# One decoder layer: the seven late shared experts in a chain, their sums beside them, and one routed tile moved to the last list

## The chip, the cores and the metric

The kernel runs on one core of a Trainium2 chip. The metric is device time in microseconds (us) from start to end of one execution. TensorE (PE in the profile) multiplies matrices. VectorE (DVE), ScalarE (ACT) and GpSimd (POOL) do elementwise work. SyncE (SP) starts most of the transfers. Each engine works through its own list of instructions in order and waits on semaphores for the others.

## The reference, cut to what matters

64 sequences of 128 positions with 256 features go through one layer. A state-space mixer and a retention-style cross-attention come first, each followed by a residual sum and a layernorm. A mixture of experts is last:

```python
shared = down(silu(x @ shared_gate) * (x @ shared_up))      # for every token
probs = sigmoid(x @ router + bias); the two best of 8 experts per token, weights scaled to sum 1
combined = sum over those two of weight * down_e(silu(x @ gate_e) * (x @ up_e))
out = layernorm(x + shared + combined)
```

Every expert has an inner width of 512. All data are float32.

## The kernel before, in words

The work is cut into 16 **groups** of four sequences (512 tokens). A group's features lie with the tokens on the partitions (`x2`, 128 x 4 x 256) and turned (`x2T`, features on the partitions).

**Routing.** `route` (L910) computes the router for a group, ranks the experts and writes each token's row twice into `xs`, a buffer in device memory with a section for each of the 8 experts. That is done with eight indirect transfers from GpSimd's queue (L992). From the counts so far `tile_list` (L1039) makes a list of **tiles**: 256 (or in the last batch 128) rows of one expert. There are 78 tiles in five batches, `BATCHES`: 9, 16 and 16 tiles are listed after groups 4, 8 and 12; 16 full tiles and 21 half tiles after the last group.

**One routed tile** (`one_tile`, L1215): `fetch` (L1134) copies the tile's list entry on GpSimd, loads its rows from `xs` and, if the expert is another one than the buffer holds, its 1.5 MB of weights, both through SyncE's queue. There are three weight buffers (`NW`). `rows_turned` (L1156) transposes the rows on TensorE, `hidden` (L1172) makes the gate and up products, and `down` (L1198) the down products. The down of tile i stands behind the hidden of tile i+1 (`waiting`), and its rows leave for `ys` by an indirect transfer from GpSimd (L1208). After the tile, `room[0] = i + NW` (L1226) lets the next tile be fetched.

**The shared expert** of a group (`shared`, L1003): four chunks of 128 inner features. Each chunk has a gate product and an up product in a PSUM bank of the pool `gu` (three banks), SiLU on ScalarE (L1015) and a multiplication on VectorE (L1016), which gives `hc`. Then come two down products, each over two sequences, also in `gu`, and an add on VectorE for each (L1024). Float32 products are two TensorE passes, so a chunk is 8 instructions in the profile, and a group is 32 (128x512) for gate and up and 32 (128x256) for down. Groups 7 to 13 (`LATE`) do it at the end (`late_shared`, L1454). The others do it earlier, and put x plus the shared part in `x2_rows`.

**The sum** (`combine`, L1230): one 1 MB load of the two routed rows of each token (`picked`, three buffers), two adds of 128x1024 on VectorE (L1239), and `layernorm` (L551): statistics on VectorE for each sequence (L557, L558), variance plus epsilon (L560), a power of -1/2 on GpSimd (L562), shift (L564), four scalings on ScalarE (L567), and a store of 512 KB (L1242).

**The order of the work** is written out by a small planner inside the kernel. `abreast` (L1247) takes several generators. Each says, at each step, where it stands (a position) and how long it should rest. The one with the lowest position that is not resting goes next. The clock, `work[0]`, counts TensorE's time by the kernel's own rates. `placed` (L1265) turns the work done and the rests into a position. There are three such runs, one after the other:

1. L1448: attention of all groups, routing, early shared experts and 41 routed tiles. `per_tick` (L1407) says how many tiles stand beside each group: four beside each of the ticks 13 to 16.
2. L1470: the other 37 tiles, padding rows for `xs` (`fill_behind`, L1100: eight indirect transfers from GpSimd, then seven from SyncE), and the shared expert of group 15.
3. L1487: the seven late shared experts (`all_shared`) beside the 16 sums (`all_sums`, L1476). The nine early groups are summed first, the seven late ones after them, in the order in which their shared parts are made. A late sum uses a tile `x2s_late` for the group.

The order of instructions on an engine is not wholly that of the code: a ready instruction can be brought forward. In the trace two products of group 7's shared expert lie in the middle of the last routed tile's down (1856.48 us).

Of the kernel before, what the change touches and what calls it, by code (L numbers as in the profile page):

```python
# [26 lines left out]
CF = FF // P  # L27
NE = 8
NF = NE + 1
GB = 4  # L30
T = GB * L
# [13 lines left out]
LATE = range(7, 14)  # L45
# [464 lines left out]
def _shared_decay(ctx, K):  # L510
    tc, nc = K.tc, K.tc.nc
    NG = K.x.shape[0] // GB
    x, ctxT, ffn, out = K.x, K.ctxT, K.ffn, K.out
    ident, mhalf, gam, bet, w_in_s, cw, cb, w_x_s = (
        K.ident, K.mhalf, K.gam, K.bet, K.w_in_s, K.cw, K.cb, K.w_x_s
    )
# [7 lines left out]
    ring = ctx.enter_context(tc.tile_pool(name="ring", bufs=3))  # L524
    tiles = ctx.enter_context(tc.tile_pool(name="tiles", bufs=2))
    small = ctx.enter_context(tc.tile_pool(name="small", bufs=4))
    dram = ctx.enter_context(tc.tile_pool(name="dram", bufs=2, space=bass.MemoryType.DRAM))
    pm = ctx.enter_context(tc.tile_pool(name="pm", bufs=5, space=bass.MemoryType.PSUM))
    gu = ctx.enter_context(tc.tile_pool(name="gu", bufs=3, space=bass.MemoryType.PSUM))
# [21 lines left out]

    def layernorm(dst, src):

        mv = small.tile([P, GB, 2], F32, name="mv")
        for b in range(GB):
            st = small.tile([P, nc.vector.BN_STATS_DIM], F32, name="st")
            nc.vector.bn_stats(st, src[:, b, :])  # L557
            nc.vector.bn_aggr(mv[:, b, :], st)  # L558
        var = small.tile([P, GB], F32, name="var")
        nc.vector.tensor_scalar(var, mv[:, :, 1], EPS, None, ALU.add)  # L560
        rstd = small.tile([P, GB], F32, name="rstd")
        nc.gpsimd.tensor_tensor(rstd, var, mhalf, ALU.pow)  # L562
        shift = small.tile([P, GB], F32, name="shift")
        nc.vector.scalar_tensor_tensor(shift, mv[:, :, 0], -1.0, rstd, ALU.mult, ALU.mult)  # L564
        yield 4.2
        for b in range(GB):
            nc.scalar.activation(  # L567
                dst[:, b, :], src[:, b, :], AF.Identity, bias=shift[:, b : b + 1], scale=rstd[:, b : b + 1]
            )
# [430 lines left out]
            nc.sync.dma_start(out=x2T_rows[g], in_=x2T.rearrange("p k t -> p (k t)"))  # L1000
        st["x2T"] = x2T

    def shared(x2, x2T, x2s):  # L1003

        wg = shared_w[:, 0:SZ].rearrange("p (k i) -> p k i", k=KD)
        wu = shared_w[:, SZ : 2 * SZ].rearrange("p (k i) -> p k i", k=KD)
        wd = shared_w[:, 2 * SZ :].rearrange("p (c h) -> p c h", c=CF)
        hid = []
        for c in range(CF):
            psg = gu.tile([P, T], F32, name="gu")  # L1010
            project(psg, wg, c * P, x2T)
            psu = gu.tile([P, T], F32, name="gu")
            project(psu, wu, c * P, x2T)
            hc = ring.tile([P, T], F32, name="hc", bufs=4)
            nc.scalar.activation(hc, psg, AF.Silu)  # L1015
            nc.vector.tensor_tensor(hc, hc, psu, ALU.mult)  # L1016
            hid.append(hc)
            yield 0.3 if c < CF - 1 else 2.0
        for j in range(GB // 2):
            ps = gu.tile([P, 2, D], F32, name="gu")  # L1020
            for i in range(2):
                b = 2 * j + i
                project_rows(ps[:, i, :], [h[:, b * L : (b + 1) * L] for h in hid], wd, slice(0, D))
            nc.vector.tensor_tensor(  # L1024
                x2s[:, 2 * j : 2 * j + 2, :], x2[:, 2 * j : 2 * j + 2, :], ps, ALU.add
            )
            yield

    def early_shared(g, st):
        yield from shared(st["x2"], st["x2T"], st["x2"])  # L1030
        nc.sync.dma_start(out=x2_rows[g].rearrange("p (b d) -> p b d", d=D), in_=st["x2"])

    def load_rows(g):
        xts.append(xts.pop(0))
        t = xts[-1]
        nc.sync.dma_start(out=t.rearrange("p b d -> p (b d)"), in_=x2_rows[g])
        return t

    def tile_list(k):  # L1039

# [188 lines left out]

    def combine(g, x2s):  # L1230

        y = late.tile([P, GB, 2, D], F32, name="picked", bufs=3)
        nc.sync.dma_start(
            out=y, in_=ys[g * GB * 2 * L : (g + 1) * GB * 2 * L, :].rearrange(
                "(b p k) d -> p b k d", p=P, k=2)
        )
        yield 1.0
        for k in range(2):
            nc.vector.tensor_tensor(x2s, x2s, y[:, :, k, :], ALU.add)  # L1239
        yield 3.0  # L1240
        yield from layernorm(x2s, x2s)
        nc.sync.dma_start(out=out[g * GB : (g + 1) * GB].rearrange("b l d -> l b d"), in_=x2s)  # L1242
        yield 3.0


# [90 lines left out]
    for side in range(2):  # L1336
# [3 lines left out]
        b0, half = 0, L // 2  # L1340
        while half >= Q:
# [4 lines left out]
            b0, half = 2 * nb, half // 2  # L1346
        ps = pm.tile([KB, P], F32, name="pm")
# [6 lines left out]
    SZ = KD * FF  # L1354
    shared_w = const.tile([P, 3 * SZ], F32, name="shared_w")
# [51 lines left out]
    per_tick = {}  # L1407
    for k, (groups, first, n, _) in enumerate(BATCHES[:-2]):
        ticks = range(groups + 1, BATCHES[k + 1][0] + 1)
        for j, t in enumerate(ticks):  # L1410
            per_tick[t] = n * (j + 1) // len(ticks) - n * j // len(ticks)
    def until(ready, at):
        while not ready():
            yield at, 0.5
# [36 lines left out]

    late = ctx.enter_context(tc.tile_pool(name="late", bufs=1))

    def late_shared(g):  # L1454
        x2 = load_rows(g)
        x2T = two.tile([P, KD, T], F32, name="x2T")
        nc.sync.dma_start(out=x2T.rearrange("p k t -> p (k t)"), in_=x2T_rows[g])
        yield 4.0
        x2s = late.tile([P, GB, D], F32, name="x2s_late", bufs=len(LATE))
        yield from shared(x2, x2T, x2s)  # L1460
        sums.append((g, x2s))

    sums = []
    def other_tiles():
        begin = listed[0]
        for i in range(begin, NT):
# [4 lines left out]
        (other_tiles(), True), (placed(fill_behind(), 0.0, 23.0, 0.25), True),  # L1471
        (placed(early_shared(NG - 1, states[NG - 1]), 0.0, 23.0, 0.15), True),
    )
    sums += [(g, None) for g in range(NG) if g not in LATE]

    def all_sums():  # L1476
        for i in range(NG):
            while not sums:
                yield i / NG, 1.0
            g, x2s = sums.pop(0)  # L1480
            yield from placed(combine(g, load_rows(g) if x2s is None else x2s), i / NG, 12.0, 1 / NG)

    def all_shared():
        for i, g in enumerate(LATE):
            yield from placed(late_shared(g), i / len(LATE), 27.0, 1 / len(LATE))

    abreast((all_shared(), True), (all_sums(), True))  # L1487

# [184 lines left out]
```

## Time and profile before

| what | value |
|---|---|
| three runs | 2025.27, 2032.85, 2033.28 us; median 2032.85 |
| the profiled execution | 2031.02 us |
| its span, first to last instruction | 2029.2 us |
| mean granted TensorE clock | 0.979 |
| TensorE busy, whole span | 1887.0 us (93%) |
| VectorE busy, whole span | 990.6 us (49%) |
| run 2 (tiles of the last list) | about 1512 to 1858 us |
| run 3 (late shared experts, sums) | about 1858 us to the end |

A view "by stretches" gives for each stretch of the span the busy time of each engine, the granted clock, the busy share of the transfer engines and their rate. A "group" is all instructions of one line, engine and operation on the same tiles, with the number of them, the time of one, and what ended the idle time before them. A "timeline" lists instructions in order of time. Its columns are start, duration, engine, line, operation, output and input, count, and in brackets the idle time before the first of them with what ended it. The "chain" is followed back from the last instruction.

### The profile page before, as it was taken

The page shows a single profiled execution, that of the slowest core. Times are in us where ns is not written, and L with a number is a line of the kernel's source. Part 1 is how long each engine was busy: PE and PEld are TensorE (multiplying, and loading weights), DVE is VectorE, ACT ScalarE, POOL GpSimd, SP SyncE. Part 2 cuts the span into 40 slices and gives each one's busy share as a digit, 9 for nine tenths or more (in the row PEclk, how much of TensorE's full clock was granted, in tenths as well). Part 3 has the DMA queues.
Part 4 walks back from the last instruction along what each step waited for, and adds up shares of the span by engine and source line. Part 5 has one row for each costly group of instructions (what it writes and reads, how often), then busy time and mean ns, then how long its engine had stood idle before and what let it go on. Part 6 is the DMA issues. An engine that isn't in the chain of part 4 may idle for free. (4 is left out here: it accounts for less than half of the span.)

```text
span 2029.2 us, 26056 instructions
## 1 busy us (share of the span) xinstructions
PE 1887.0 (93%) x9252; PEld 1402.0 (69%) x9252; DVE 990.6 (49%) x2400; ACT 757.6 (37%) x1248; POOL 466.7 (23%) x699
## 2 busy tenths in 40 slices
PE   4889998999999979999999899999997999899996
PEld 2655666686868657767777677777775888787553
DVE  3666676655555564555555555554440111012574
ACT  4355344343334434444535353525221222222332
POOL 3021221230303121313131222222223222222110
PEclk9899999999999989999999999999998999999999
DMA  4111121420404142512331342322114332443772
GB/s 145 28 55 44 45 73 34 159 72 23 135 26 133 54 146 75 177 54 83 92 100 54 125 136 95 96 94 75 53 52 164 127 120 71 167 159 124 252 269 79
DMA packets 96308, 206.40 MB, mean 102 GB/s; under 512 B 22344, under 2 KB 59848, under 8 KB 91048
## 3 DMA queue, kind: packets, MB, share of 16 engines
q1 hardware_dynamic: 73048, 149.37, 22.8%
q0 software_dynamic: 17616, 52.46, 7.6%
q10 hardware_dynamic: 5504, 2.81, 0.5%
q8 instruction: 75, 1.23, 0.3%
q14 instruction: 65, 0.53, 0.1%
HBM read 207.33 MB, written 58.60 MB: 131 GB/s over the span
## 5 line engine op out<-in xcount | busy, mean ns | idle before, releaser
L543 PE MATMUL gu<-rows_T,routed_w 128*128 128x256 f32 (+1 forms) x2496 | 504.4, 355 | 15.6 <-DMA routed_w<-in_ffn_dram 15.5
L543 PEld LDWEIGHTS gu<-rows_T,routed_w 128*128 128x128 f32 x2496 | 421.1, 193 | 79.7 <-issue 30.3
L1192 DVE TENSOR_TENSOR hid<-hid,gu 128x512 f32<-128x512 f32 x135 | 92.5, 685 | 395.9 <-PE gu L543 327.6
L543 PE MATMUL pm<-routed_w,hid 128*128 128x256 f32 x1080 | 259.2, 386 | 0.3 <-issue 0.2
L543 PE MATMUL pm<-xnT,w_in_s 128*128 128x512 f32 x512 | 242.8, 599 | 5.2 <-ACT xnT L580 2.6
L543 PE MATMUL gu<-x2T,shared_w 128*128 128x512 f32 x512 | 229.9, 595 | 1.2 <-DVE hc L1016 1.2
L1208 POOL DMA_INDIRECT ys<-rows_out,to x135 | 138.2, 1024 | 380.7 <-ACT rows_out L1207 327.4
L543 PEld LDWEIGHTS pm<-routed_w,hid 128*128 128x128 f32 x1080 | 200.7, 193 | 27.7 <-issue 3.3
L628 DVE SCALAR_TENSOR_TENSOR xc<-pm,cw,xc 128x508 f32<-128x508 f32 (+2 forms) x192 | 141.0, 740 | 68.4 <-ACT xc L623 65.4
L543 PEld LDWEIGHTS gu<-x2T,shared_w 128*128 128x128 f32 x512 | 94.8, 190 | 108.9 <-issue 101.7
L543 PEld LDWEIGHTS pm<-xnT,w_in_s 128*128 128x128 f32 x512 | 96.0, 193 | 91.2 <-issue 76.4
L567 ACT ACTIVATE x<-x,shift,rstd 128x256 f32<-128x256 f32 x132 | 70.7, 591 | 202.3 <-DVE shift L564 202.3
L562 POOL TENSOR_TENSOR rstd<-var,mhalf 128x4 f32<-128x4 f32 x64 | 68.3, 1068 | 330.1 <-DVE var L560 166.5
L1191 ACT ACTIVATE hid<-gu 128x512 f32<-128x512 f32 x135 | 80.4, 596 | 152.1 <-PE gu L543 135.7
L1207 ACT ACTIVATE rows_out<-pm,wt 128x256 f32<-128x256 f32 x135 | 58.0, 472 | 189.6 <-PE pm L543 168.8
L543 PE MATMUL gu<-shared_w,hc 128*128 128x256 f32 x512 | 117.0, 382 | 7.4 <-DVE hc L1016 7.3
L543 PE MATMUL pm<-w_out_s,sz 128*128 128x256 f32 x512 | 117.0, 382 | 4.3 <-DVE sz L784 3.8
L543 PEld LDWEIGHTS gu<-shared_w,hc 128*128 128x128 f32 x512 | 95.7, 190 | 28.6 <-DVE hc L1016 11.8
L543 PEld LDWEIGHTS pm<-w_out_s,sz 128*128 128x128 f32 x512 | 95.8, 190 | 25.9 <-DVE sz L784 7.6
L992 POOL DMA_INDIRECT xs<-x,index x64 | 66.7, 1042 | 174.0 <-issue 78.8
L623 ACT ACTIVATE xc<-pm,cb,cw 128x512 f32<-128x512 f32 x64 | 49.7, 777 | 117.9 <-PE pm L543 117.9
L640 ACT ACTIVATE sz<-pm 128x512 f32<-128x512 f32 x64 | 37.9, 594 | 113.1 <-PE pm L543 113.1
(234 smaller groups left out, 2511.9 us busy)
## 6 DMA issues: line engine op xcount, KB each, us to landing
routed_w<-in_ffn_dram SPq DMA_DIRECT2D x78, 1536.0 KB
picked<-ys SPq DMA_DIRECT2D x16, 1024.0 KB
rows_in<-xs SPq DMA_DIRECT2D x57, 258.0 KB
cT<-in_ctxT_dram POOLq DMA_DIRECT2D x16, 512.0 KB
cq<-chunks SPq DMA_DIRECT2D x16, 512.0 KB
x_rows<-x SPq DMA_DIRECT2D x16, 512.0 KB
xt<-in_x_dram POOLq DMA_DIRECT2D x10, 512.0 KB
xt<-x_rows SPq DMA_DIRECT2D x10, 512.0 KB
```

What stands on the lines that cost most here:

```text
L543: nc.tensor.matmul(out, lhsT=lhsT, rhs=rhs, **how)
L562: nc.gpsimd.tensor_tensor(rstd, var, mhalf, ALU.pow)
L567: nc.scalar.activation(dst[:, b, :], src[:, b, :], AF.Identity, bias=shift[:, b : b + 1], scale=rstd[:, b : b + 1])
L623: nc.scalar.activation(xcf[:, c, :], ps, AF.Identity, bias=cb[:, c : c + 1], scale=cw[:, c, TAPS - 1 : TAPS],)
L628: nc.vector.scalar_tensor_tensor(xc[:, c, :, s:], ps3[:, :, : L - s], cw[:, c, TAPS - 1 - s : TAPS - s], xc[:, c, :, s:], ALU.mult, ALU.add,)
L640: nc.scalar.activation(sz[:, c, :], ps, AF.Silu)
L992: s = nc.gpsimd.indirect_dma_start(out=xs, in_=rows[k][:, b, :], in_offset=None, out_offset=bass.IndirectOffsetOnAxis(ap=index[:, b, k : k ...
L1191: nc.scalar.activation(hc, psg, AF.Silu)
L1192: nc.vector.tensor_tensor(hc, hc, psu, ALU.mult)
L1207: nc.scalar.activation(y[:, j, :], ps[:, j, :], AF.Copy, scale=wt[:, j : j + 1])
L1208: s = nc.gpsimd.indirect_dma_start(out=ys, in_=y[:, j, :], in_offset=None, out_offset=bass.IndirectOffsetOnAxis(ap=to[:, j : j + 1], axis=0),)
```

## The change

`layernorm` takes any number of sequences. `shared` is cut in two: `shared_hidden`, which makes the four chunks, and `shared_down`, which makes the down products in a pool of banks that is given to it. In run 3 the down of a late group is written after the second chunk of the next late group, in the pool `pm` (five banks) instead of `gu`; the last group's own down follows its last chunk. The two adds of the routed rows of a late group are written ahead of its down, on `x2_late`. The layernorm and the store of a late group are done for two sequences at a time (so two of each, with 256 KB stores). The routed rows of a late group are loaded at its second chunk. Its `x2` and `x2T` are loaded one group ahead. `all_sums` keeps only the nine early groups, spread over all of run 3. The hidden tiles of the late groups have six buffers of their own instead of four. Last, `per_tick[NG] -= 1`: three tiles instead of four stand beside tick 16, so that run 2 begins with tile 40, which belongs to the third batch of full tiles and whose rows and weights are fetched under the earlier list, and has 38 tiles.

```diff
     def layernorm(dst, src):
-        mv = small.tile([P, GB, 2], F32, name="mv")
-        for b in range(GB):
+        n = src.shape[1]
+        mv = small.tile([P, GB, 2], F32, name="mv")[:, 0:n, :]
+        for b in range(n):
...
-    def shared(x2, x2T, x2s):
+    def shared_hidden(x2T, pool, bufs):
         wg = shared_w[:, 0:SZ].rearrange("p (k i) -> p k i", k=KD)
         wu = shared_w[:, SZ : 2 * SZ].rearrange("p (k i) -> p k i", k=KD)
-        wd = shared_w[:, 2 * SZ :].rearrange("p (c h) -> p c h", c=CF)
         hid = []
         for c in range(CF):
             psg = gu.tile([P, T], F32, name="gu")
             project(psg, wg, c * P, x2T)
             psu = gu.tile([P, T], F32, name="gu")
             project(psu, wu, c * P, x2T)
-            hc = ring.tile([P, T], F32, name="hc", bufs=4)
+            hc = pool.tile([P, T], F32, name="hc", bufs=bufs)
             nc.scalar.activation(hc, psg, AF.Silu)
             nc.vector.tensor_tensor(hc, hc, psu, ALU.mult)
             hid.append(hc)
-            yield 0.3 if c < CF - 1 else 2.0
+            yield 0.3
+        return hid
+
+    def shared_down(x2, hid, x2s, banks):
+        wd = shared_w[:, 2 * SZ :].rearrange("p (c h) -> p c h", c=CF)
         for j in range(GB // 2):
-            ps = gu.tile([P, 2, D], F32, name="gu")
+            ps = banks.tile([P, 2, D], F32, name=banks.name)
...
+            yield j
+
+    def early_shared(g, st):
+        hid = yield from shared_hidden(st["x2T"], ring, 4)
+        yield 1.7
+        for _ in shared_down(st["x2"], hid, st["x2"], gu):
             yield
...
+    def load_products(g):
+        y = late.tile([P, GB, 2, D], F32, name="picked", bufs=3)
+        nc.sync.dma_start(out=y, in_=ys[...])
+        return y
+
+    def store(g, x2s, b0, b1):
+        nc.sync.dma_start(
+            out=out[g * GB + b0 : g * GB + b1].rearrange("b l d -> l b d"), in_=x2s[:, b0:b1, :]
+        )
...
     def combine(g, x2s):
-        y = late.tile([P, GB, 2, D], F32, name="picked", bufs=3)
...
-        yield 1.0
+        y = load_products(g)
+        yield 4.0
         for k in range(2):
             nc.vector.tensor_tensor(x2s, x2s, y[:, :, k, :], ALU.add)
-        yield 3.0
         yield from layernorm(x2s, x2s)
-        nc.sync.dma_start(out=out[g * GB : (g + 1) * GB].rearrange("b l d -> l b d"), in_=x2s)
+        store(g, x2s, 0, GB)
         yield 3.0
...
             per_tick[t] = n * (j + 1) // len(ticks) - n * j // len(ticks)
+    per_tick[NG] -= 1
...
-    def late_shared(g):
-        x2 = load_rows(g)
+    def late_shared(g, last):
+        if not loaded:
+            load_late(g)
+            yield 4.0
+        x2, x2T = loaded.pop()
+        if not last:
+            load_late(g + 1)
+        made = shared_hidden(x2T, late, 6)
+        for c in range(CF):
+            yield next(made)
+            if c == 1:
+                y = load_products(g)
+                if unsummed:
+                    yield from summed(*unsummed.pop())
+        try:
+            next(made)
+        except StopIteration as end:
+            hid = end.value
+        unsummed.append((g, x2, y, hid))
+        if last:
+            yield 1.7
+            yield from summed(*unsummed.pop())
+
+    def summed(g, x2, y, hid):
+        for k in range(2):
+            nc.vector.tensor_tensor(x2, x2, y[:, :, k, :], ALU.add)
+        norms = []
+        for j in shared_down(x2, hid, x2, pm):
+            norms.append((j, layernorm(x2[:, 2 * j : 2 * j + 2, :], x2[:, 2 * j : 2 * j + 2, :])))
+            next(norms[-1][1])
+            yield 0.5
+        for j, norm in norms:
+            for _ in norm:
+                pass
+            store(g, x2, 2 * j, 2 * j + 2)
+        yield
+
+    def load_late(g):
         x2T = two.tile([P, KD, T], F32, name="x2T")
         nc.sync.dma_start(out=x2T.rearrange("p k t -> p (k t)"), in_=x2T_rows[g])
-        yield 4.0
-        x2s = late.tile([P, GB, D], F32, name="x2s_late", bufs=len(LATE))
-        yield from shared(x2, x2T, x2s)
-        sums.append((g, x2s))
+        x2 = late.tile([P, GB, D], F32, name="x2_late", bufs=4)
+        nc.sync.dma_start(out=x2.rearrange("p b d -> p (b d)"), in_=x2_rows[g])
+        loaded.append((x2, x2T))
...
     def all_sums():
-        for i in range(NG):
-            while not sums:
-                yield i / NG, 1.0
-            g, x2s = sums.pop(0)
-            yield from placed(combine(g, load_rows(g) if x2s is None else x2s), i / NG, 12.0, 1 / NG)
+        for i, g in enumerate(early):
+            yield from placed(combine(g, load_rows(g)), i / len(early), 12.0, 1 / len(early))

     def all_shared():
         for i, g in enumerate(LATE):
-            yield from placed(late_shared(g), i / len(LATE), 27.0, 1 / len(LATE))
+            yield from placed(late_shared(g, g == LATE[-1]), i / len(LATE), 25.0, 1 / len(LATE))
```

More of the change, by code (lines that the diff above doesn't have):

```diff
@@ L558, in layernorm @@
             nc.vector.bn_aggr(mv[:, b, :], st)
-        var = small.tile([P, GB], F32, name="var")
+        var = small.tile([P, GB], F32, name="var")[:, 0:n]
         nc.vector.tensor_scalar(var, mv[:, :, 1], EPS, None, ALU.add)
-        rstd = small.tile([P, GB], F32, name="rstd")
-        nc.gpsimd.tensor_tensor(rstd, var, mhalf, ALU.pow)
-        shift = small.tile([P, GB], F32, name="shift")
+        rstd = small.tile([P, GB], F32, name="rstd")[:, 0:n]
+        nc.gpsimd.tensor_tensor(rstd, var, mhalf[:, 0:n], ALU.pow)
+        shift = small.tile([P, GB], F32, name="shift")[:, 0:n]
         nc.vector.scalar_tensor_tensor(shift, mv[:, :, 0], -1.0, rstd, ALU.mult, ALU.mult)
         yield 4.2
-        for b in range(GB):
+        for b in range(n):
             nc.scalar.activation(
@@ L1026, in shared @@
             )
+            yield j
[3 more added lines that the diff above has]
+        for _ in shared_down(st["x2"], hid, st["x2"], gu):
             yield
-    def early_shared(g, st):
-        yield from shared(st["x2"], st["x2T"], st["x2"])
         nc.sync.dma_start(out=x2_rows[g].rearrange("p (b d) -> p b d", d=D), in_=st["x2"])
@@ L1037, in load_rows @@
         return t
+    def load_products(g):
+        y = late.tile([P, GB, 2, D], F32, name="picked", bufs=3)
+        nc.sync.dma_start(
+            out=y, in_=ys[g * GB * 2 * L : (g + 1) * GB * 2 * L, :].rearrange(
+                "(b p k) d -> p b k d", p=P, k=2)
+        )
+        return y
+    def store(g, x2s, b0, b1):
+        nc.sync.dma_start(
+            out=out[g * GB + b0 : g * GB + b1].rearrange("b l d -> l b d"), in_=x2s[:, b0:b1, :]
+        )
     def tile_list(k):
@@ L1230, in combine @@
     def combine(g, x2s):
-        y = late.tile([P, GB, 2, D], F32, name="picked", bufs=3)
[L1233 to L1236, printed above, removed]
-        yield 1.0
+        y = load_products(g)
+        yield 4.0
         for k in range(2):
             nc.vector.tensor_tensor(x2s, x2s, y[:, :, k, :], ALU.add)
-        yield 3.0
         yield from layernorm(x2s, x2s)
-        nc.sync.dma_start(out=out[g * GB : (g + 1) * GB].rearrange("b l d -> l b d"), in_=x2s)
+        store(g, x2s, 0, GB)
         yield 3.0
@@ L1452, in _shared_decay @@
     late = ctx.enter_context(tc.tile_pool(name="late", bufs=1))
-    def late_shared(g):
-        x2 = load_rows(g)
+    def late_shared(g, last):
[33 more added lines that the diff above has]
+        yield
+    unsummed, loaded = [], []
+    def load_late(g):
         x2T = two.tile([P, KD, T], F32, name="x2T")
         nc.sync.dma_start(out=x2T.rearrange("p k t -> p (k t)"), in_=x2T_rows[g])
-        yield 4.0
-        x2s = late.tile([P, GB, D], F32, name="x2s_late", bufs=len(LATE))
-        yield from shared(x2, x2T, x2s)
-        sums.append((g, x2s))
-    sums = []
+        x2 = late.tile([P, GB, D], F32, name="x2_late", bufs=4)
+        nc.sync.dma_start(out=x2.rearrange("p b d -> p (b d)"), in_=x2_rows[g])
+        loaded.append((x2, x2T))
     def other_tiles():
@@ L1473, in _shared_decay @@
     )
-    sums += [(g, None) for g in range(NG) if g not in LATE]
+    early = [g for g in range(NG) if g not in LATE]
     def all_sums():
-        for i in range(NG):
-            while not sums:
-                yield i / NG, 1.0
-            g, x2s = sums.pop(0)
-            yield from placed(combine(g, load_rows(g) if x2s is None else x2s), i / NG, 12.0, 1 / NG)
+        for i, g in enumerate(early):
+            yield from placed(combine(g, load_rows(g)), i / len(early), 12.0, 1 / len(early))
     def all_shared():
         for i, g in enumerate(LATE):
-            yield from placed(late_shared(g), i / len(LATE), 27.0, 1 / len(LATE))
+            yield from placed(late_shared(g, g == LATE[-1]), i / len(LATE), 25.0, 1 / len(LATE))
     abreast((all_shared(), True), (all_sums(), True))
```

## The prediction

> **What bounds the kernel now.** I read the stretches first, because the change touches three stages with different limits.
>
> ```profile
> span 2029.2 us, 26056 instructions
> ...
> 1433.00:1512.00 79.00, 78.78 (x356) 60.32 (x355) 33.54 (x81) 20.80 (x38) 9.76 (x13) 1.00 0.11 34
> 1527.00:1540.00 13.00, 5.05 (x17) 4.13 (x18) 0.69 (x1) 1.33 (x3) 2.68 (x5) 0.66 0.87 325
> 1559.00:1570.00 11.00, 6.36 (x27) 5.18 (x26) 0.69 (x1) 0.84 (x2) 3.18 (x8) 0.94 0.66 216
> 1858.00:2014.00 156.00, 147.34 (x452) 84.56 (x450) 89.38 (x221) 47.38 (x89) 19.66 (x17) 1.00 0.63 221
> 2014.00:2029.00 15.00, 0.34 (x2) 0.00 (x0) 5.23 (x13) 2.07 (x4) 1.01 (x1) 0.68 0.12 40
> ```
>
> After the times the first number is TensorE's busy time, the third VectorE's. The last group's attention (1433 to 1512) is full of TensorE work. At the passage to the last list TensorE idles twice. In the late experts it is busy nearly throughout, and the last 15 us have none of it. The timeline of TensorE places the idle time.
>
> ```profile
> 1529.78 0.66 PE L547 MATMUL pm<-ident,rows_in 128*128 128x128 f32 x4 [3.74 <-DMA rows_in<-xs]
> 1535.61 1.09 PE L547 MATMUL pm<-ident,rows_in 128*128 128x128 f32 x4 [5.17 <-DMA rows_in<-xs]
> 1537.34 9.10 PE L543 MATMUL gu<-rows_T,routed_w 128*128 128x256 f32 x32
> ...
> 1568.35 5.38 PE L543 MATMUL gu<-rows_T,routed_w 128*128 128x256 f32 x16 [4.64 <-DMA routed_w<-in_ffn_dram]
> ```
>
> It waits for the first tiles' rows, works slowly afterwards (9.10 us for what takes 7.07 later), and waits for weights. In the late stage the groups of instructions say what TensorE and VectorE wait for:
>
> ```profile
> L543 PE MATMUL gu<-x2T,shared_w 128*128 128x512 f32 x224 | 98.1, 593 | 1.2 <-DVE hc L1016 1.2
> L543 PE MATMUL gu<-shared_w,hc 128*128 128x256 f32 x224 | 51.3, 383 | 7.4 <-DVE hc L1016 7.3
> L564 DVE SCALAR_TENSOR_TENSOR shift<-mv,rstd 128x4 f32<-128x4 f32 x16 | 2.6, 163 | 15.2 <-POOL rstd L562 15.2
> ```
>
> The down products wait for the last hidden chunk, which VectorE makes late. The end is read from the chain:
>
> ```profile
> 1987.82 26.53 PE gu L543 x90
> ...
> 2014.37 0.70 DVE x2s_late L1024
> ...
> 2015.10 1.24 DVE x2s_late L1239
> ...
> 2019.76 1.00 POOL rstd L562
> ...
> 2021.49 1.57 ACT x2s_late L567 x3
> ```
>
> **Part one, the tail.** From the last product (2014.35) to the span's end are 14.85 us: add of the shared part 0.70, two adds of routed rows 2.48, statistics of four sequences 1.77 (2017.61 to 2019.38), variance to the start of the power 0.36, power 1.00, shift 0.20, four scalings 2.1, store and end 6.1. After the change the routed rows are added before the down, and only two sequences remain: 0.70 + 0.89 + 0.36 + 1.00 + 0.20 + 1.08. The other half's VectorE work (0.70 + 0.89 + 0.17 + a wait of 1.2 for the power + 0.16 = 3.1) fits behind the second down (16 products 0.216 apart, 3.45). The 512 KB store moved its bytes between 2024.0 and 2025.7, so half of it saves 0.85: 5.25. The sum is 9.5, a gain of 5.3; with a late first half 3.5.
>
> **Part two, the late stage.** Undisturbed, 32 gate and up products take 13.74 us (1925.59 to 1939.33) and 32 down products 6.9. Seven groups are 144.5, less 0.86 for two products done earlier: 143.6. From 1859.06 to 2014.35 are 155.3, so 11.7 are lost. In three groups the gate part took longer than 13.74 (by 0.78, 1.64 and 0.35): 2.8 lost there. The other 8.9 are lost at the downs. (The rows charge 8.6 in all; the rest is in starts after a wait.) With the down behind two chunks of the next group, its last hidden tile has 16 x 0.43 = 6.9 us more; the latest in the trace was late by some 2 us behind six products that could go. So 8.9 falls to nothing; the last group has no cover, but it lost nothing before either.
>
> What comes instead: seven more round trips to GpSimd. One leaves VectorE idle 15.2/16 = 0.95 and adds a variance and a shift of 0.16 each: 7 x 1.28 = 9.0. Behind such a wait stand the multiplications that free `gu` banks, and TensorE is who waits for these; it has about 2.5 us before a bank is missed. VectorE has room: busy 89, waiting for GpSimd or transfers some 29, for TensorE the other 40. So far 29 us of such waits cost 2.8 at the gates, and 9.0 more would cost 0.9. I take 1.5; the ends are 0 and 9. The gain is 7.4. The down's banks cost nothing, since `pm` is idle in this stage. `picked` is a tighter place: a late group's rows may occupy one of three buffers for a group (20 us). Two are left for nine sums in 145 us, 16 us each, and loads landed in 5 to 8. Half stores double SyncE's issues there by seven, 0.38 each, but each waits for its scalings with the loads behind it.
>
> Here a rule speaks against the change. The Trainium skill ("SBUF — State Buffer", Who interferes with whom) says that a VectorE instruction with two inputs in SBUF and a GpSimd instruction that reads SBUF block each other for a whole instruction. The routed adds are of that kind, and so is the power. The trace agrees: three of 16 powers lasted 1.8 to 1.95 instead of 1.0. By the row, 23 powers meet an add 23 x 3/16 times, which is 1.3 us more than before on VectorE and little on TensorE. By the rule at its worst, each of the seven new ones meets an add: 7 x 1.22 = 8.5, and at the same exchange (2.8/29) 0.8 on TensorE: 6.6 instead of 7.4. I keep the row's.
>
> **Part three, the kept tile.** Tile 40 is 32 gate and up products (6.9), 16 down (3.45) and a transposition (0.44), 10.8 us of TensorE. It moves from before the count product (1511.69, call it W) to behind it; its rows and weights are on hand. TensorE was full before W, so W comes 10.8 earlier if nothing needed the tile as cover. The count was ready at 1503.2, and its product ran at 1507.8, behind tile 40's: the routing waited for the tile. After the change 7 us of work (half a shared down, a tile's down) remain for its 5.8 us of VectorE; were only the 3.6 there, 2.2 would be lost.
>
> After W the data set the pace: eight scatters on GpSimd, rows at W + 18.1, weights of tile 41 by W + 25.6, of tile 43 at W + 56.6. The last load was issued at 1560.33, behind padding writes in SyncE's queue that wait for GpSimd. TensorE's work up to there is 39.2 (shared gate and up 13.7, three transpositions 1.3, gate and up of two tiles 13.8, two downs 6.9, half a shared down 3.45), the rest idle or slow; 10.8 more make 50.0, still under 56.6. So tile 43 begins at W + 56.6 in both, and the gain is the 10.8 of W, less what the order spoils. Two things can: the transposition of tile 41 now stands in the middle of tile 40 by the planner's clock (it expects rows at W + 12), and if engines keep that order TensorE stands from W + 6.9 to W + 18.1, with 43 us of work to go: W + 61.2, a loss of 4.6. And the weights of tile 42 take the buffer of tile 39, whose down is now behind tile 40: at W + 25 in that case, landed by W + 33 and needed at W + 36, with `rows_in` and weights of 43 behind them in SyncE's queue. Ends: a loss of 6.8, or a gain of 4 more if weights 43 pass the padding. I take a loss of 3.3, half of the bad end: gain 7.5.
>
> **Sum.** 5.3 + 7.4 + 7.5 = 20.2. Against the profiled execution: 2031.0 - 20.2 = 2010.8. The median of the runs shown is 1.8 above that execution, so in its terms 2032.85 - 20.2 = 2012.7, which is the forecast.
>
> **Rivals.** (1) The passage gives nothing: idle in the last attention, or TensorE standing before tile 41, eats the 10.8. For it: the idle rows above are waits for data, which a tile doesn't bring sooner. Against: W moves only if TensorE's list shortens, and that was full. Gain 12.7: 2020. (2) VectorE bounds the late stage, each new round trip reaching TensorE: stage gain 0, so again 12.8, 2020. For it: 1.64 lost at the gates of one group where sums crowded. Against: its 40 us of room. (3) Slower: the early sums starve. SyncE's queue is in order; a store or a `picked` load waiting for its buffer holds all loads behind it, and sums slip behind the last expert. One sum moves 2.1 MB; at the 280 GB/s of the busiest stretch (1950 to 1975) it costs 7.5 us there. Three left over undo the gain of 20.2 (22.5: 2035); from the third on it is slower. Against: nine sums over the stage, transfers busy 0.63. (4) The change doesn't act: instructions are brought forward already, so that the order may come out as before: 2032.
>
> **Chances.** All three pay (2005 to 2018, from the ends above): 0.62. Rival 1: 0.17, rival 2: 0.10, rival 3: 0.06, rival 4: 0.05. Within 0.5% is what a measurement of this kernel can hardly tell from no change (the runs shown differ by 0.4%): faster means under 2022.7. Of the first case all counts, of rivals 1 and 2 some seven in ten: 0.81. Slower is rival 3 and a little of 1: 0.07. The rest, 0.12, is the same. The range, 2004 to 2024, holds the first case and the middle of the next two.
>
> **What would show it.** Tail: no routed add and two scalings after the last product, some 9.5 us. Late stage: no `hc` wait at the down products, groups 20.7 to 21.2 us apart; gate waits over 5 us would show rival 2, sums after the last product rival 3. Passage: the count product near 1501; TensorE's waits for `rows_in` gone or before tile 40's second half; the first 128-row tiles some 8 us earlier. The prediction is wrong if the count product doesn't move, or if VectorE's waits reach the gate products.

## The result and the profile after

The changed kernel takes 2018.15 us (median of seven runs, 2015.99 to 2027.28), the kernel before 2033.28 beside it (seven runs, 2025.27 to 2036.89). The ratio is 0.9935, with a 95% interval of 0.9914 to 0.9957. The medians differ by 15.1 us, the profiled spans by 14.1 (2029.2 to 2015.1). The forecast was a gain of 20.2.

To see where the 14.1 lie, I cut each span at three marks that exist in both traces: the start of the last group's last row of `w_out` products, the **count product** W that closes the routing, and the end of the last routed down, where the late experts begin. A fourth mark is the end of the last product.

| stretch, us | before | after | gain | forecast |
|---|---|---|---|---|
| start to last `w_out` product | 1436.98 | 1438.03 | -1.05 | 0 |
| from there to W | 74.71 | 64.22 | 10.49 | 10.8 |
| W to the end of the last routed down | 347.38 | 350.77 | -3.39 | -3.3 |
| late experts, to the last product | 155.27 | 152.55 | 2.7 | 7.4 |
| tail, to the end of the span | 14.86 | 9.53 | 5.3 | 5.3 |

So four of five rows are as forecast. Three quarters of the shortfall of 6.1 lie in one row, the late experts. (That the third row fits is in part luck, as the experiments show.) The stretches of the profile after (us, then TensorE, its weight loads, VectorE, ScalarE, GpSimd busy, clock, transfer share, GB/s):

```profile
1438.00:1502.00 64.00, 64.00 (x292) 48.82 (x291) 26.02 (x63) 17.12 (x31) 7.36 (x10) 1.00 0.10 35
1513.00:1524.00 11.00, 1.40 (x5) 0.55 (x4) 0.69 (x1) 0.60 (x1) 6.30 (x13) 0.77 0.36 111
1853.00:2005.60 152.60, 145.93 (x447) 83.88 (x445) 94.56 (x241) 47.80 (x90) 25.01 (x23) 1.00 0.61 212
2005.60:2015.10 9.50, 0.00 (x0) 0.00 (x0) 1.99 (x7) 1.73 (x4) 0.70 (x1) 0.75 0.19 64
```

TensorE is full up to W, as it was. It stands for 10 us behind W, and in the late stage it is idle for 6.7 of 152.6 us, though no row says yet for what. The tail is 9.5 us with seven VectorE instructions. The groups of the late stage name the wait (1850 to 2016 us, different shapes kept apart):

```profile
L543 PE MATMUL gu<-x2T,shared_w 128*128 128x512 f32 x224 | 99.6, 596 | 6.6 <-DVE hc L1016 3.3 <-ACT hc L1015 3.3
L543 PE MATMUL pm<-shared_w,hc 128*128 128x256 f32 x224 | 49.5, 379 | 0.0
L563 POOL TENSOR_TENSOR rstd<-var,mhalf 128x4 f32<-128x4 f32 x9 | 14.2, 1574 | 44.7 <-DVE var L561 44.7
L563 POOL TENSOR_TENSOR rstd<-var,mhalf 128x2 f32<-128x2 f32 x14 | 10.6, 755 | 83.9 <-DVE var L561 59.8 <-DVE mv L559 24.1
L565 DVE SCALAR_TENSOR_TENSOR shift<-mv,rstd 128x2 f32<-128x2 f32 x14 | 2.2, 161 | 8.6 <-POOL rstd L563 8.6
L565 DVE SCALAR_TENSOR_TENSOR shift<-mv,rstd 128x4 f32<-128x4 f32 x9 | 1.5, 163 | 8.5 <-POOL rstd L563 8.5
```

The 7.4 us at the down products are gone. The gate and up products, which had waited 1.2, now wait 6.6, half of it for VectorE's multiplication and half for ScalarE's SiLU. The timeline shows one such place, at the first late group's down (start, duration, engine; in brackets the idle time before):

```profile
1877.77 1.22 DVE L1257 TENSOR_TENSOR xt<-xt,picked 128x1024 f32<-128x1024 f32 x1
1877.94 1.91 POOL L563 TENSOR_TENSOR rstd<-var,mhalf 128x4 f32<-128x4 f32 x1 [7.67 <-DVE var L561]
...
1879.88 0.16 DVE L565 SCALAR_TENSOR_TENSOR shift<-mv,rstd 128x4 f32<-128x4 f32 x1 [0.90 <-POOL rstd L563]
...
1883.67 0.16 DVE L565 SCALAR_TENSOR_TENSOR shift<-mv,rstd 128x2 f32<-128x2 f32 x1 [0.22 <-POOL rstd L563]
...
1883.87 1.09 ACT L568 ACTIVATE x_late<-x_late,shift,rstd 128x256 f32<-128x256 f32 x2 [1.71 <-DVE shift L565]
...
1884.87 0.57 ACT L1015 ACTIVATE hc<-gu 128x512 f32<-128x512 f32 x1
...
1885.49 1.98 PE L543 MATMUL gu<-x2T,shared_w 128*128 128x512 f32 x4 [0.52 <-ACT hc L1015]
```

It is a chain over four engines. A power on GpSimd lasts 1.91 beside a routed add, and VectorE's shift stands behind it. The add of the down, statistics and a second trip to GpSimd follow, and only then the shift at 1883.67. ScalarE's scalings, after 1.71 idle, wait for that shift. The SiLU that frees a bank of `gu` stands behind the scalings, and TensorE waits for the bank. The passage behind W reads:

```profile
1502.25 0.59 PE L543 MATMUL pm<-count,ones 128*128 128x8 f32 x4
1502.69 1.97 PE L543 MATMUL gu<-rows_T,routed_w 128*128 128x256 f32 x8
...
1523.73 1.12 PE L547 MATMUL pm<-ident,rows_in 128*128 128x128 f32 x4 [9.60 <-DMA rows_in<-xs]
1524.64 5.84 PE L543 MATMUL pm<-routed_w,hid 128*128 128x256 f32 x16
1530.32 2.74 PE L543 MATMUL gu<-x2T,shared_w 128*128 128x512 f32 x6
...
1561.45 7.14 PE L543 MATMUL gu<-rows_T,routed_w 128*128 128x256 f32 x32
```

The transposition of tile 41 stands in TensorE's list before a down, a part of the shared expert and the rest of what was ready. It waits 9.60 us for its rows, which landed at W + 21.5. Tile 43 begins at W + 59.2 (before: W + 56.7), now without a wait. From there to the last routed down, before and after:

```profile
1568.35:1859.20 290.85, 279.84 (x1641) 253.08 (x1642) 34.41 (x50) 66.81 (x133) 70.19 (x157) 0.99 0.35 119
1561.45:1853.20 291.75, 280.91 (x1658) 253.71 (x1658) 35.09 (x51) 66.53 (x135) 69.95 (x157) 1.00 0.36 123
```

The granted clock was 0.99 before and 1.00 after, which matters below.

### The profile page after: what moved, and what is told of

It reads as the page before. It is cut to its first block, busy times and chain, and to the rows that moved or that the text cites. A ratio compares the mean times of both kernels' runs of the same rounds, so it can differ in the third digit from the quotient of the medians.

```text
span 2015.1 us, 26110 instructions
## 1 busy us (share of the span) xinstructions
PE 1884.6 (94%) x9252; PEld 1400.2 (69%) x9252; DVE 990.3 (49%) x2414; ACT 756.8 (38%) x1248; POOL 473.9 (24%) x706
## 4 chain that ended last, share of the span: by engine, by line
PE 65%; DVE 10%; issue 10%; DMA 5%; ACT 4%; POOL 2%; another core or an unknown queue 0%; SPq 0%; ACTq 0%; POOLq 0%; DVEq 0%
PE pm L543 36%; PE gu L543 25%; PE pm L547 4%; POOL rstd L563 1%; DMA x_rows<-x 1%; DMA routed_w<-in_ffn_dram 1%; DMA picked<-ys 1%; DMA cq<-chunks 1%; DVE xc L782 1%; ACT L694 1%; ACT x L568 1%; POOL ys L1230 1%; DVE sz L785 1%; DVE st L558 1%; DVE hid L1214 1%
## 5 line engine op out<-in xcount | busy, mean ns | idle before, releaser
L543 PEld LDWEIGHTS gu<-rows_T,routed_w 128*128 128x128 f32 x2496 | 416.5, 191 | 72.9 <-issue 21.2
L568 ACT ACTIVATE x<-x,shift,rstd 128x256 f32<-128x256 f32 x140 | 74.8, 591 | 211.1 <-DVE shift L565 211.1
L563 POOL TENSOR_TENSOR rstd<-var,mhalf 128x4 f32<-128x4 f32 (+1 forms) x71 | 74.4, 1047 | 332.8 <-DVE var L561 166.3
L782 DVE SCALAR_TENSOR_TENSOR xc<-xc,dsk,pm 128x512 f32<-128x512 f32 x64 | 47.3, 742 | 62.7 <-PE pm L543 40.4
L543 PE MATMUL pm<-mt,xd 128*128 128x128 f32 x512 | 69.5, 286 | 4.2 <-ACT xn L568 2.4
```

The source lines that it names most:

```text
L543: nc.tensor.matmul(out, lhsT=lhsT, rhs=rhs, **how)
L563: nc.gpsimd.tensor_tensor(rstd, var, mhalf[:, 0:n], ALU.pow)
L568: nc.scalar.activation(dst[:, b, :], src[:, b, :], AF.Identity, bias=shift[:, b : b + 1], scale=rstd[:, b : b + 1])
L782: nc.vector.scalar_tensor_tensor(y, xcf[:, c, :], dsk[:, c : c + 1], ps.rearrange("p b l -> p (b l)"), ALU.mult, ALU.add)
```

## The experiments

The runs fall into three sets; the first and the third ran on one chip, the second on another. The start of the span, which hardly any edit touches, differs by some ten us between the two, so I compare within a set, and by stretches of the trace. The kernel before had medians of 2016.66, 2034.34 and 2018.33 us beside the three sets. The stretches of all runs:

| run | ratio to before (95%) | last `w_out` to W | W to last routed down | late stage | tail |
|---|---|---|---|---|---|
| set 1: without the kept tile | 0.9970 (0.9958 to 0.9983) | 74.72 | 349.5 | 152.71 | 9.66 |
| kept tile alone | 0.9973 (0.9960 to 0.9987) | 64.22 | 357.6 | 154.35 | 14.96 |
| up products in other banks | 0.9937 (0.9917 to 0.9957) | 64.22 | 355.5 | 150.55 | 9.50 |
| no power | 0.9930 (0.9911 to 0.9950) | 64.22 | 359.0 | 146.15 | 8.42 |
| set 2: after, again | 0.9959 (0.9940 to 0.9978) | 64.22 | 354.2 | 153.35 | 9.53 |
| whole norms | 0.9949 (0.9930 to 0.9967) | 64.28 | 350.4 | 149.98 | 10.57 |
| rows later | 0.9983 (0.9967 to 0.9998) | 64.21 | 363.5 | 154.48 | 9.55 |
| both of these | 0.9967 (0.9952 to 0.9982) | 64.22 | 361.4 | 151.14 | 10.81 |
| set 3: zeros from GpSimd | 0.9965 (0.9945 to 0.9986) | 64.23 | 360.9 | 151.92 | 10.05 |
| zeros, rows later | 0.9972 (0.9957 to 0.9987) | 64.22 | 354.4 | 152.93 | 10.26 |
| zeros, rows later, whole norms | 0.9952 (0.9934 to 0.9970) | 64.22 | 354.7 | 150.71 | 9.94 |
| these three and the banks | 0.9906 (0.9887 to 0.9924) | 64.22 | 357.7 | 144.71 | 10.07 |

### The kept tile and the rest apart

The kernel after without its last step, and the kernel before with that step alone:

```diff
-    per_tick[NG] -= 1
```

> Four tiles beside tick 16 again, the late stage and the tail as changed. If the three parts add up as the two traces say (passage 6.1, late stage 2.7, tail 5.3 us), the count product runs near 1511.7 us, the late stage lasts 152.6 us from the last routed down to the last product, the tail 9.5, and the span is 2015.1 + 6.1 = 2021.2 (gain over before 8.0, ratio 0.996). If instead the passage gives nothing by itself and the gain of 6.1 came from a shift of other work, the span stays near 2015.

```diff
+    per_tick[NG] -= 1
```

> Kernel before with only per_tick[NG] -= 1. By the same sum: count product near 1502, late experts begin near 1853, late stage 155.3 and tail 14.9 as before, span 2029.2 - 6.1 = 2023.1 (ratio 0.997). If the order of the late stage is what makes the passage good or bad (loads for it brought forward into the passage), it differs from that by more than 2 us.

Without the kept tile the ratio is 0.9970, some 6 us; its two stretches say 7.8 against the trace of before (late stage 155.27 to 152.71, tail 14.86 to 9.66). The kept tile alone gives 0.9973, some 5.4 us (2.6 to 8.1). The product of both ratios is 0.994, between the two measurements of the whole change (0.9935 and 0.9959), so the parts add, as far as these intervals can tell. W moves by the same 10.5 us wherever the tile is kept. What it costs behind W varies: 3.4 in the traces of the result, 8.1 in this set (349.5 to 357.6), 6.0 and 9.5 in the other two runs of the set.

Part of this lies ahead of tile 43. It starts at W + 56.7 before, at W + 58.4 without the kept tile, and at W + 58.9 to W + 61.8 in the six traces that keep the tile and after's order of transpositions and padding. That hardly depends on how much work TensorE has till then, because data sets it: in two of the six (after and whole norms) the rows of tile 41, for which TensorE stands 9.6 us, in the others at the end the weights of tile 43 (waits of 1.2 to 4.7 us). What is left of the difference lies behind: from tile 43 to the last routed down the six take 291.6 to 298.5 us, and the longer they take, the lower is the granted clock there (1.00 in after, 0.98 in the longest).

### The late up products in the banks of `pm`

```diff
-    def shared_hidden(x2T, pool, bufs):
+    def shared_hidden(x2T, pool, bufs, second=gu):
...
-            psu = gu.tile([P, T], F32, name="gu")
+            psu = second.tile([P, T], F32, name=second.name)
...
-        made = shared_hidden(x2T, late, 6)
+        made = shared_hidden(x2T, late, 6, pm)
```

> After, with the up products of the late groups in the five banks of pm (gate products keep gu's three); VectorE's list keeps its order. Theory 'late, not full': VectorE and ScalarE make hidden tiles 1 to 3 us late in bursts, and three banks can't bridge that; with more banks TensorE runs on, its waits at gate products fall from 8.7 to 1 to 3 us, late stage 145 to 147, span near 2009. Rival 'full': VectorE is the bound of the stage, banks only move the wait (to the down products or to the banks a group later): late stage 151 to 153, span near 2015.

The late stage takes 150.55, against 152.71 in the same set, which is between the cases. The difference alone says little, since one and the same late stage took 151.9 to 154.5 us in the six traces of after and of runs that don't edit it. The waits say more. (The expectations speak of 8.7 us at the gate products; the groups of after show 6.6.) The groups of this run (1849 to 2010 us):

```profile
L543 PE MATMUL pm<-x2T,shared_w 128*128 128x512 f32 x112 | 52.6, 592 | 0.0
L543 PE MATMUL gu<-x2T,shared_w 128*128 128x512 f32 x110 | 51.8, 592 | 0.0
L543 PE MATMUL pm<-shared_w,hc 128*128 128x256 f32 x224 | 51.7, 389 | 4.5 <-DVE hc L1016 4.5
```

No gate or up product waits any more. The wait has gone to the down products of two groups (2.33 and 2.21 us). More banks let TensorE run ahead, and then it meets VectorE's lateness itself.

### No power in the sums

The norms of the third run of the planner leave out the power, so that the scale is the variance plus epsilon; nothing goes to GpSimd and back there.

```diff
-        rstd = small.tile([P, GB], F32, name="rstd")[:, 0:n]
-        nc.gpsimd.tensor_tensor(rstd, var, mhalf[:, 0:n], ALU.pow)
+        if own:
+            rstd = var
+        else:
+            rstd = small.tile([P, GB], F32, name="rstd")[:, 0:n]
+            nc.gpsimd.tensor_tensor(rstd, var, mhalf[:, 0:n], ALU.pow)
```

> After, with the power left out in run 3's 23 layernorms (the scale is the variance plus epsilon itself), so no round trip to GpSimd there; everything else is done. Theory 'round trips': the 23 waits of VectorE for GpSimd (17.1 us) put hidden tiles behind them, on VectorE and through the scalings on ScalarE; without them TensorE's waits at gate products fall from 8.7 to under 3, late stage 145 to 147, the tail shortens by about 1.1 to 8.4, span near 2008. Rival 'the adds and the early sums': VectorE's own work in front of the hidden tiles is what delays them: late stage 150 or more, span 2012 to 2014 (tail gain and a part).

```profile
L543 PE MATMUL gu<-x2T,shared_w 128*128 128x512 f32 x222 | 97.5, 594 | 1.3 <-DVE hc L1020 0.9 <-ACT hc L1019 0.2
L543 PE MATMUL pm<-shared_w,hc 128*128 128x256 f32 x224 | 49.5, 379 | 0.0
```

The late stage falls to 146.15, 6.6 us less than in the same set, and the wait at the gates to 1.3, about what it was before the change. The tail takes 8.42, as expected. So the round trips to GpSimd, 23 instead of 16, are what TensorE waits for in the end. The edit takes away the trips together with their meetings with routed adds, which are looked at below.

### Whole norms

The late groups, the last excepted, are normed and stored all four sequences at a time, as before the change. That is six round trips fewer, with the down still behind the next group's chunks.

```diff
+        if g != LATE[-1]:
+            for j in shared_down(x2, hid, x2, pm):
+                yield 0.5
+            for _ in layernorm(x2, x2):
+                pass
+            store(g, x2, 0, GB)
+            yield
+            return
```

> The changed kernel once more, beside the next three on the same chip. Late stage 152 to 153 us, tail 9.5, TensorE's wait for the first rows of the last list 8 to 10.

> After, with the layernorm and the store of the late groups done whole again (four sequences, one power, one store) for all but the last; the last keeps its halves. Six round trips to GpSimd fewer (17 instead of 23). Theory 'all round trips alike': leaving out all 23 gave 6.4 us, so six give 1.7: late stage near 150.9, tail 9.5. Rival 'the halves are the culprits': they stand back to back ahead of the hidden tiles after each down; then most of the 6 us come back: late stage 147 to 148. Third: nothing, 152 to 153, since a whole norm has the same adds and statistics, and its power waits for both downs.

After again, and whole norms:

```profile
L543 PE MATMUL gu<-x2T,shared_w 128*128 128x512 f32 x222 | 98.8, 596 | 7.2 <-ACT hc L1015 3.9 <-DVE hc L1016 3.2
L543 PE MATMUL gu<-x2T,shared_w 128*128 128x512 f32 x222 | 98.0, 595 | 4.6 <-DVE hc L1016 3.0 <-ACT hc L1015 1.6
```

The late stage takes 149.98, 3.4 less than after's 153.35 beside it; the gate waits fall from 7.2 to 4.6. So about half of the 6.6 goes with the six added trips, and it is paid back in part by a tail that is 1.0 longer.

### The rows of tile 41 expected later

The planner takes them to be there 22 us after the fetch, not 12. The transposition is then behind the ready work.

```diff
-            there.append(work[0] + 12.0)
+            there.append(work[0] + (22.0 if fetched[0] == BATCHES[3][1] else 12.0))
```

> After, with the planner's estimate for the rows of tile 41 raised from 12 to 22 us of work; in TensorE's list tile 40, its predecessor's down and all of group 15's gate and up products then stand ahead of tile 41's transposition (24 us of work), and the half tiles keep the order of before. Theory 'the data set the pace' (as in the prediction): the wait for rows goes from 8 to 10 to under 4, but TensorE then waits for the weights of tile 43, which are issued behind the padding at about W + 50: from the count product to the late stage only 1 to 4 us less than in the changed kernel. Rival 'order alone': the whole wait is gained, 9 us less or more.

> The two edits together. If they don't meet, the gains add: with the middle guesses 1.7 + 2.5 = 4 us under the changed kernel on this chip; at best 5 + 9.

It takes 9 us more behind W than after beside it (363.5 against 354.2). TensorE no longer stands at the transposition, and stands longer two tiles on:

```profile
1531.73 0.66 PE L547 MATMUL pm<-ident,rows_in 128*128 128x128 f32 x4 [2.35 <-DMA rows_in<-xs]
...
1572.90 5.98 PE L543 MATMUL gu<-rows_T,routed_w 128*128 128x256 f32 x16 [15.90 <-DMA routed_w<-in_ffn_dram]
```

The weights of tile 43 are issued at W + 62.2, behind four padding writes in SyncE's queue, where after issues them at W + 50.9. With the whole norms added, the late stage gains 3.3 once more and the wait stays (15.70).

### The padding writes out of SyncE's queue

The prediction held these writes to be what keeps the weights back. So they go to GpSimd's queue, first in the order of after, then with the later rows, with the whole norms, and with the banks:

```diff
-                s = nc.sync.dma_start(out=xs[row : row + P, :], in_=zeros)
+                s = nc.gpsimd.dma_start(out=xs[row : row + P, :], in_=zeros)
```

> After, with the seven zero-filling writes of the padding issued from GpSimd's queue instead of SyncE's; the order of the transpositions is after's. Theory (the padding writes, ahead of the weights of tile 43 in SyncE's queue, set when those weights come; the rows come late on their own): the weights of tile 43 are issued some 10 to 15 us earlier and no product waits for them, but in after that wait was only 0 to 1.2 us and a wait of 9.5 for the rows of tile 41 remains: the time from the count product to the end of the last routed down falls by 0 to 2 us against after's 350.8 and 354.2. Rival (the bandwidth of the DMA engines sets both): the weights come no earlier. Second rival (GpSimd's queue is now longer, the copies of the normed rows stand behind the zeros): the wait for the rows grows by 1 to 4 us and the time by as much.

> The run that transposes the kept tile's successor later (the planner takes its rows to be there after 22 instead of 12), with the seven zero-filling writes in GpSimd's queue. Theory (the rows wait and the weights wait are two separate ones; with the zeros out of the weights' queue the later transposition pays): waits for the rows at most 4 us, none or under 3 us at the gates of tile 43 (15.9 with the zeros in SyncE's queue), count product to the end of the last routed down 340 to 346 us, some 8 less than after on the same kind of chip (350.8 and 354.2). Rival (whatever is moved, the transfers of the passage end at the same time): the wait comes back at tile 43 or at the next tile, and the time is 350 to 355.

> The same with the last groups' norms over the whole group at once, except the last group's, as in the run of whole norms. Theory: passage as in the run before this one (340 to 346), late stage 150 to 151 instead of 152.6 to 153.4, tail 10.6: the time 1.5 to 2.5 us below that of the run before. Rival (the norms' round trips don't matter while other waits do): the same time within 0.5 us.

> The same with the up products of the last groups in the banks of the sums, as in the run of the banks alone. Theory (banks and round trips are two ways to lose the same waits, and each alone left 150): the late stage falls to 146 to 149, as it stood at 146.2 without the powers; the time is 2 to 4 us below the run before. Rival (what is left is VectorE's own work in this stage): 150 to 151 as with either alone, and the time is the same.

The theory of the two waits fell. In after's order the weights of tile 43 come no earlier (W + 55.5), and from W to the last routed down it takes 360.9 us, longer than in both traces of after. With the later rows the weights are issued at W + 54.6 instead of W + 62.2, and the wait at tile 43 is 12.22, where it was 15.90 in the second set. So the writes in SyncE's queue are worth some 3.7 us of that wait, and something else the rest. The ratios of the two runs (0.9965 and 0.9972) are no better than after's. SyncE's waits in the run with zeros and later rows, then in that with later rows alone (1500 to 1600 us: in total, times, longest), and GpSimd's timeline in the first of them name it:

```profile
SPq L1162 <- POOL rows_in L1161: 50.0, 5, 24.2
...
SPq L1137 <- POOL rows_in L1161: 23.9, 1, 23.9
```

```profile
1531.43 1.08 POOL L1131 DMA_INDIRECT xs<-zeros,behind_i  x1 [0.50 <-POOL zeros L1127]
1534.41 0.22 POOL L1127 TENSOR_SCALAR zeros<-zeros 128x1 f32<-128x1 f32 x1 [1.90 <-DMA xs<-zeros,behind_i]
1534.91 1.05 POOL L1131 DMA_INDIRECT xs<-zeros,behind_i  x1 [0.28 <-POOL zeros L1127]
1537.85 0.21 POOL L1127 TENSOR_SCALAR zeros<-zeros 128x1 f32<-128x1 f32 x1 [1.90 <-DMA xs<-zeros,behind_i]
1538.37 0.64 POOL L1137 DMA_DIRECT2D xs<-zeros  x1 [0.30 <-POOL zeros L1127]
1539.00 0.30 POOL L1161 COPY rows_in<-what 1x3 int32<-1x3 int32 x2
```

Each padding write needs `zeros` to be changed first, and that waits for the write before to land. Behind these steps, in the same queue, stand small copies of list entries (L1161), from which SyncE reads which rows and which weights to fetch. They are not tile 43's own: SyncE had read that entry and started the rows at W + 22.8. They are those of the next two tiles, and SyncE's reads of them stand in its list ahead of the weights of tile 43. The copies come at W + 49.2, and SyncE has waited 24.2 us for them, although tile 40's down, which frees the buffer for these weights, ended at W + 37.5. In the run with later rows alone the same copies came at W + 49.8, and SyncE waited 23.9 us there too, at the first padding write in its own queue (L1137). That write waits for a change of `zeros` that stands behind the same steps on GpSimd and ended at W + 49.9, just before the write went (the view names the copy beside it). So the padding does hold the weights back, but by its steps on GpSimd. Taking the writes out of SyncE's queue only moved SyncE's wait from a write to a read. A run with the copies ahead of the padding, or on another engine, was not made, so what this would give stays open.

The second half of the last set answers for the late stage. The whole norms take 2.2 us off it, and the banks on top 6.0 more: 144.71, where the banks alone had given 2.2.

```profile
L543 PE MATMUL pm<-x2T,shared_w 128*128 128x512 f32 x112 | 52.6, 592 | 0.0
L543 PE MATMUL gu<-x2T,shared_w 128*128 128x512 f32 x110 | 51.8, 592 | 0.0
L543 PE MATMUL pm<-shared_w,hc 128*128 128x256 f32 x224 | 49.9, 380 | 0.5 <-DVE hc L1016 0.5
```

TensorE waits 0.5 us in the whole stage, and the stage is 1.1 from the 143.6 of undisturbed products. This run is the fastest of the study: 2000.27 us (four runs, 1996.78 to 2006.75), where before stood at 2018.33.

## Why the prediction was right, and where it was not

**The tail: right to 0.1 us.** No routed add and two scalings follow the last product. The chain of after, read from the end:

```profile
2005.61 0.70 DVE x_late L1029
...
2006.33 0.75 DVE st L558 x2
...
2007.70 0.69 POOL rstd L563
...
2009.11 0.58 ACT x_late L568
```

The power was put at 1.00 and took 0.69, for two columns instead of four. The steps ahead of it took 0.18 more than put and the store with the end 0.16 more, which evened it out. The first half was not late.

**The passage: the move of W right, the loss behind it right in part by luck.** "W comes 10.8 earlier" was 10.5. "I take a loss of 3.3, half of the bad end" was 3.4 in the traces of the result. But the six traces with the tile kept in this order took 350.4 to 359.0 us behind W, the two without it 347.4 and 349.5: the middles differ by 6.4, close to the whole bad end of 6.8. The result's trace is one of the two shortest of the six, in which the granted clock behind the start of tile 43 was 1.00. The change measured again (second set) gave a ratio of 0.9959, a gain of 8.3 us (4.5 to 12.2) where the result has 15.1.

The order that came is the bad case as described: the transposition stands by the planner's clock in front of ready work. It stood 9.60 us where 11.2 had been put. "Tile 43 begins at W + 56.6 in both" holds to 5.1 us over the eight traces. Of the signs, the missing waits for `rows_in` did not show, and that one was badly chosen: it belonged to the good case, not to the one that the loss was taken from. The first half tiles came 5.1 us earlier (1724.5 to 1719.4), not 8. That rows landed 3.4 us later behind W was not foreseen. The scatters stood behind two of `ys` and one of padding, which the earlier count had passed: W moved by 10.5, the scatters' end by 7.2. The reason given for the late weights, "behind padding writes in SyncE's queue that wait for GpSimd", names the right engine in its last words: it is the steps on GpSimd that hold SyncE, with or without these writes in its queue. The end "a gain of 4 more if weights 43 pass the padding" was not had by moving the writes.

**The late stage: here the prediction failed, at one term.** "8.9 falls to nothing" was right: the down products wait 0.0. The new waits were the miss: "9.0 more would cost 0.9. I take 1.5; the ends are 0 and 9". With undisturbed products at 143.6, the gate part's excess in after is 152.5 - 143.6 = 8.9, where 2.8 had been before, so the seven added trips and what goes with them cost 6.1. That is 4.6 over the term, and the late stage's shortfall is 4.7. Both factors were off. VectorE's waits for the power grew only from 15.2 us (16 shifts) to 17.1 (8.6 and 8.5 in the two kinds), not by seven times 0.95, so what each of these us cost TensorE was far more than put. The exchange rate was wrong: I took 2.8/29, an average over waits of which most stood where nobody needed the next instruction. The added ones stand right after the down, two in a row, with the routed adds of an early sum among them and SiLU behind the scalings. "About 2.5 us before a bank is missed" was the right scale, but several waits add up inside one such stretch. The run without powers shows that the loss hangs on the round trips, and the whole norms that six of the added ones are about half of it. The banks show what TensorE misses first: a bank, and the hidden chunk itself once banks are there.

The second rival, in which each new trip reaches TensorE, described the mechanism. The sign set for it, gate waits over 5 us, came true (6.6), and so did one of the two signs by which the prediction called itself wrong: VectorE's waits reached the gate products. It put the stage's gain at 0 and the time at 2020, nearer to 2018.15 than the forecast's 2012.7. It was wrong in the cause, "VectorE bounds the late stage": VectorE is busy 94.6 of 152.6 us, and with one arrangement of banks and norms the same VectorE work fits into 144.7. What bounded it was the order in which waits stand, and too few banks to bridge them.

**The shared port.** Of 23 powers, the row of before made 23 x 3/16 = 4.3 slow ones. By the rule of the Trainium skill ("SBUF — State Buffer", Who interferes with whom) at its worst, the seven new ones would all have met an add, on top of the three of before: ten. The trace has seven, of 1.51 to 1.95 us. Each of the seven lies beside a routed add for about 1 us, and no other power does, so the rule fits the trace. But the added trips are hardly among them: six of the nine whole norms of the early groups met an add, and one of the fourteen halves (the groups above show means of 1574 and 755 ns). Three further traces of the same late stage have five slow powers instead of seven and took 152.7, 152.9 and 154.5 us, against 151.9 to 153.4 with seven. Two slow powers fewer thus made no visible difference; what all seven cost, no run separates.

The starved sums of the third rival did not show: no sum and no routed add came after the last product. Nor did the fourth: W moved, and the downs stand behind the next chunks.

## What to carry to other kernels

A wait added on a helper engine is not priced by the average of such waits. It is priced by what stands behind it on each engine in the place where it is put, and waits that stand close together add up against one small supply of buffers. When a wait moves on in spite of two edits, look for the queue in which the *address* of a transfer is made, its own or that of one issued ahead of it, not only the queue that issues it. And two cures that look alike (more banks, fewer round trips) can each give little alone and nearly everything together: 2.2 us and 2.2 to 3.4 us one at a time, 8.2 together, where traces of one and the same late stage differed by up to 2.6.

## What the runs showed of the hardware

The power on GpSimd takes 0.70 us for two columns and 1.01 for four when nothing disturbs it, so halving a norm doubles the trips and saves 0.3 of each; beside a two-input add of 1024 elements on VectorE it took up to 1.95. The stretch up to the last `w_out` product, which is nearly the same in all runs, took 1421 to 1430 us on the chip of the first and third sets and 1435 to 1439 in the others; two profiled executions on one chip, of kernels that are alike up to the late stage, differed by 5.8 us (1422.04 and 1427.86). Differences of that size in a whole time say nothing of an edit. The stretches say more, though they vary too: from W to the last routed down by 8.6 us over the six traces in one order, and in one and the same late stage by 2.6.
